# First cross attention: transposed blocks sent through DRAM to their partitions

## The chip, the cores and the metric

The kernel runs on one core of a Trainium2 chip. The core has a matrix engine (TensorE, "PE" in the profile, with its weight loads shown apart as "PEld"), a vector engine (VectorE, "DVE"), a scalar engine (ScalarE, "ACT"), GpSimd ("POOL") and a queue engine (SyncE, "SP") that here only starts transfers. Sixteen DMA engines move the data between DRAM and the on-chip memory SBUF, and within SBUF. SBUF has 128 partitions; a tile of 128 x n elements has n elements in each partition.

The metric is the device time in microseconds. All arithmetic is in float32.

## The reference, cut to what matters

The program is two layers of a perceiver for 16 batches of 64 latent tokens (256 features) that attend to 1024 context tokens per batch. The change touches the first of six blocks, the cross attention of the first layer:

```python
q = jnp.einsum('bsd,dhe->bshe', inputs_q, Wq) + bq      # latents, 64 per batch, 16 heads of 64
k = jnp.einsum('bsd,dhe->bshe', inputs_kv, Wk) + bk     # context, 1024 per batch
v = jnp.einsum('bsd,dhe->bshe', inputs_kv, Wv) + bv
q = q / jnp.sqrt(jnp.asarray(HD, dtype=q.dtype))
scores = jnp.einsum('bqhd,bkhd->bhqk', q, k)
weights = jax.nn.softmax(scores, axis=-1)
ctx = jnp.einsum('bhqk,bkhd->bqhd', weights, v)
out = jnp.einsum('bqhd,hde->bqe', ctx, Wo) + bo
```

Five more blocks follow: a self attention, a small feed-forward block, a second cross attention, a second self attention and a mixture of experts.

## The kernel before

**How the block is tiled.** The keys are never formed: the key weights are multiplied into the queries (`absorb`), so that a score is a product of a query tile with the raw context. A step `s` treats one pair of heads of one batch: 64 latents x 2 heads fill the 128 rows, 1024 context tokens are the columns. There are 8 pairs and 16 batches, so 128 steps. In the same way the values are never formed: the probabilities are multiplied with the raw context (`gather`), and the value weights follow later (`values`).

**One step.** `scores(s)` issues four matmuls (128 x 512 each, tile `x_s` in PSUM), the row maximum (`nmax_x`, L577, DVE), the shift (L581, DVE) and the exponential with its row sum (`pr_x`, L584, ACT). `turn_probs(s)` divides by the sum (L177 and L178, DVE) and transposes within blocks of 32 x 32 (`x_pb`, L593, DVE).

**Why blocks have to move.** `gather` needs the probabilities with the context tokens on the partitions. The vector transpose turns each 32 x 32 block where it stands: what belongs to the partitions 32j to 32j+31 still lies in the partitions 32a to 32a+31, for each of the 4 x 4 pairs (a, j). So after every second step a *pair* w = (2w, 2w+1) of steps is complete in one tile `x_pb` of 128 x 2048 elements (1 MB), and 16 transfers of 64 KB, started by SP at L599, take every block from its 32 partitions to its 32 others, into the tile `x_pT`. `gather(w, c)` then runs 8 matmuls (128 x 256) for each half c of the features: 16 matmuls that read `x_pT` and the context, into `x_po`. There are 64 pairs, so 1024 such transfers.

**The context itself** is transposed in the same manner once for each batch: `turn_context` runs four vector transposes (L547, two for each half of the tokens) into `x_cb`, and 16 transfers of 64 KB (L553) take the blocks into `ctxT`, which `scores` reads. Batch 0 is an exception: PE transposes it (`first_context`). So there are 15 x 16 = 240 transfers here.

**Buffers.** `ctxT` and `x_pT` have two buffers each. `x_cb` and `x_pb` share a pool with two buffers (tag "blocks"). `x_s` has two buffers in PSUM, `x_po` one.

**What sets the order.** In the code a step issues, in this order: `turn_probs(s)`, `scores(s + 1)`, half a `gather` of the pair before, then pieces of `turn_context`, of the next tile's queries, and of the small later stages (self attention and feed-forward of a tile of two batches that is already finished; `small_stages`). That is not the order in which an engine runs them: a scheduler places every instruction on its engine's queue from costs that it estimates itself, except for those that `pin` holds in program order. Each engine then works off its queue in order. An instruction that waits holds everything behind it on that engine. In the second cross attention and what follows, the matmuls are pinned.

**SP's queue** holds nearly all transfers of this block: context loads (L197, two of 512 KB for each batch), the 16 transfers for each `x_pT` and the 16 for each `ctxT`. The weights are loaded from POOL's queue.

Of the kernel before, what the change touches and what calls it, by code (L numbers as in the profile page):

```python
# [8 lines left out]
F32 = mybir.dt.float32  # L9
# [4 lines left out]
P = 128  # L14
# [3 lines left out]
NC = D // P  # L18
N = 1024
NKT = N // P  # L20
# [26 lines left out]
def kernel(  # L47
# [30 lines left out]
    nc = tc.nc  # L78
# [18 lines left out]
    def matmul(*args, **kwargs):  # L97
        ins = nc.tensor.matmul(*args, **kwargs)  # L98
        return pin(ins) if in_order else ins

    def transpose(*args, **kwargs):
        ins = nc.tensor.transpose(*args, **kwargs)  # L102
        return pin(ins) if in_order else ins

    def bank(shape, name):
        return ps.tile(shape, F32, tag="p", name=name)

    def copy(n, dst, src):

        if n % 2:  # L110
            nc.scalar.copy(dst, src)
        else:
            nc.vector.tensor_copy(dst, src)
# [61 lines left out]
    def soft_norm(pr, total, key):  # L175
        inv = small.tile([P, 1], F32, tag="inv", name=f"inv_{key}")
        nc.vector.reciprocal(inv, total)  # L177
        nc.vector.tensor_scalar(pr, pr, inv, None, ALU.mult)  # L178
# [275 lines left out]
    st = ExitStack()  # L454
    two = st.enter_context(tc.tile_pool(name="x_two", bufs=2))
    qkp = st.enter_context(tc.tile_pool(name="x_qk", bufs=3))
    one = st.enter_context(tc.tile_pool(name="x_one", bufs=1))
    ps_s = st.enter_context(tc.tile_pool(name="x_ps_s", bufs=2, space=bass.MemoryType.PSUM))
    ps_o = st.enter_context(tc.tile_pool(name="x_ps_o", bufs=1, space=bass.MemoryType.PSUM))
# [4 lines left out]
    ctxT, qT, qk, kb, pT, acc, pct, oT, probs, blocks = ({} for _ in range(10))  # L464
# [59 lines left out]

    def first_context(g):

        if g == 0:
            ctxT[0] = two.tile([P, NC, 4, NKT, 32], F32, tag="ctxT", name="ctxT_0")  # L530
        h, c = g // 2, g % 2
        src = ctx_tiles[0][h]
        pt = bank([P, 4, P], f"ctxT_0_{g}")
        for k in range(4):
            transpose(pt[:, k, :], src[:, k, c * P : (c + 1) * P], ident)
        for k in range(4):
            copy(g, ctxT[0][:, c, :, 4 * h + k, :], pt[:, k].rearrange("p (a s) -> p a s", a=4))

    def turn_context(b, h):

        if h == 0:
            ctxT[b] = two.tile([P, NC, 4, NKT, 32], F32, tag="ctxT", name=f"ctxT_{b}")
            blocks["c"] = two.tile([P, 4, NC, NKT, 32], F32, tag="blocks", name=f"x_cb_{b}")
        cb = blocks["c"]
        src = ctx_tiles[b][h].rearrange("p k (c j s) -> p k c j s", c=NC, s=32)
        for c in range(NC):
            nc.vector.transpose(  # L547
                cb[:, :, c, 4 * h : 4 * h + 4, :].rearrange("p j k s -> p k j s"), src[:, :, c]
            )
        if h == 1:  # L550
            for a in range(4):
                for j in range(4):
                    nc.sync.dma_start(  # L553
                        out=ctxT[b][32 * j : 32 * j + 32, :, a],
                        in_=cb[32 * a : 32 * a + 32, j],
                    )

    def context_stats(b, k):

# [4 lines left out]
    def scores(s):  # L564
        b, i = divmod(s, NPAIR)
        t, u = divmod(b, 2)
        sc = ps_s.tile([P, N], F32, tag="s", name=f"x_s_{s}")
        for n in range(2):
            for c in range(NC):
                matmul(  # L570
                    sc[:, n * 512 : (n + 1) * 512],
                    lhsT=qk[t, u][:, c, 2 * i : 2 * i + 2, :].rearrange("p h q -> p (h q)"),
                    rhs=ctxT[b][:, c, 2 * n : 2 * n + 2].rearrange("p a k s -> p (a k s)"),
                    start=(c == 0), stop=(c == NC - 1),
                )
        nmax = small.tile([P, 1], F32, tag="nmax", name=f"nmax_x_{s}")
        nc.vector.tensor_reduce(nmax, sc, AX.X, ALU.max, negate=True)  # L577

        add = kb[t][:, u, i : i + 1]
        shift = small.tile([P, 1], F32, tag="shift", name=f"shift_x_{s}")  # L580
        nc.vector.scalar_tensor_tensor(shift, nmax, add, add, ALU.subtract, ALU.add)  # L581
        pr = two.tile([P, N], F32, tag="pr", name=f"pr_x_{s}")
        total = small.tile([P, 1], F32, tag="total", name=f"total_x_{s}")
        nc.scalar.activation(pr, sc, AF.Exp, bias=shift, scale=1.0, accum_out=total)  # L584
        probs[s] = pr, total

    def turn_probs(s):
        pr, total = probs.pop(s)
        soft_norm(pr, total, f"x_{s}")
        w, i = divmod(s, 2)  # L590
        if i == 0:
            blocks[w] = two.tile([P, 4, 2, NKT, 32], F32, tag="blocks", name=f"x_pb_{w}")
        nc.vector.transpose(blocks[w][:, :, i], pr.rearrange("p (j k s) -> p j k s", j=4, s=32))  # L593
        if i == 1:
            pT[w] = two.tile([P, 4, 2, NKT, 32], F32, tag="pT", name=f"x_pT_{w}")
            pb = blocks.pop(w)
            for a in range(4):
                for j in range(4):
                    nc.sync.dma_start(  # L599
                        out=pT[w][32 * j : 32 * j + 32, a], in_=pb[32 * a : 32 * a + 32, j]  # L600
                    )

    def gather(w, c):

# [71 lines left out]
    for g in range(4):  # L676
        first_context(g)
    absorb(0, 0)
    absorb(0, 1)
    first_bias(0)  # L680
    scores(0)
    queries(0, 1)
    pieces = prepare()
    for s in range(NSTEP):
        b, i = divmod(s, NPAIR)
# [3 lines left out]
        if s == NSTEP - PER_TILE + 2:  # L689
# [4 lines left out]
                out=wqo4[:, 0, :].rearrange("p (c n) -> p c n", c=NC),  # L694
                in_=l_wq.rearrange("(c p) n -> p c n", p=P),
            )
            nc.gpsimd.dma_start(
                out=wqo4[:, 1, :].rearrange("p (c n) -> p c n", n=D),
                in_=l_wo.rearrange("(c p) n -> p c n", p=P),
            )  # L700
            raw = {hh: load_half(cpool, hh // 2, hh % 2, "l_ctx") for hh in range(2)}
        if s == NSTEP - 6:
# [4 lines left out]
                cshift, cshift, -1.0, crstd, ALU.mult, ALU.mult  # L707
            )
        turn_probs(s)
        if s + 1 < NSTEP:  # L710
            scores(s + 1)
        if s >= 2:
            gather((s - 2) // 2, s % 2)
        if b + 1 < B and i in (1, 2):
            turn_context(b + 1, i - 1)
# [45 lines left out]
    with ExitStack() as st:  # L761
        one = st.enter_context(tc.tile_pool(name="l_one", bufs=1))
        two = st.enter_context(tc.tile_pool(name="l_two", bufs=2))
# [23 lines left out]
        cnT, kT, qT, vlat, pT, pct, oT, probs = ({} for _ in range(8))  # L787
# [439 lines left out]
        for qq in range(2):  # L1227
            turn_context(qq)
        issue_one()
        turn_latents(0)  # L1230
        for qq in range(2, 4):
            turn_context(qq)
# [4 lines left out]
        keys(2)  # L1237
        issue_one()
        scores(0)
        soften(0, 0)  # L1240
        keys(1)
# [8 lines left out]
        for s in range(NSTEP):  # L1250
# [3 lines left out]
            elif s + 1 < NSTEP:  # L1254
                scores((s + 1) // 2)
            turn_probs(s)
            self_steps(s, early=True)
            if s + 1 < NSTEP:
# [47 lines left out]
    with ExitStack() as st:  # L1306
        one = st.enter_context(tc.tile_pool(name="m_one", bufs=1))
        two = st.enter_context(tc.tile_pool(name="m_two", bufs=2))
# [108 lines left out]
        for n in range(2):  # L1417
            pt = bank([NE, 4, P], f"m_st_{n}")
# [16 lines left out]
        for e in range(NE):  # L1435
            w1, w2 = experts.pop(e)
            h = two.tile([P, NF, P], F32, tag="h", name=f"m_h_{e}")
# [10 lines left out]
            for n in range(2):  # L1448
                pb = bank([P, 512], f"m_pb_{e}_{n}")
                matmul(  # L1450
                    pb, lhsT=k6[0:NE, K6_SEL + e * P : K6_SEL + (e + 1) * P],
                    rhs=slotT[:, n * 512 : (n + 1) * 512], start=True, stop=True,
# [182 lines left out]
```

## Time and profile before

| | us |
|---|---|
| median of 3 runs | 2244.39 (2239.78 to 2245.81) |
| the profiled execution, its own time | 2241.03 |
| its span, first to last instruction | 2239.3 |
| first cross attention, first to last `gather` matmul | 51.2 to 1152 |
| PE busy over the span | 2144.6 (96%) |
| DVE, ACT, POOL busy over the span | 1265.6, 851.2, 310.4 |

Durations are taken from the one profiled execution. "Busy" of PE is modelled and includes the overlap of matmuls that follow each other. In the groups, one 128 x 512 float32 matmul of the code appears as two records, as does every other float32 matmul; "x1024" of `x_s` is 512 matmuls. In a row of a timeline the first column is the start, the second how long the merged group lasted, and the bracket at the end says for how long the engine had been idle and what ended it. A row of windows gives the stretch, its length, and the busy time of PE, PEld, DVE, ACT and POOL with their instruction counts, then the granted TensorE clock, the mean busy share of the DMA engines and the GB/s that they moved.

### The profile page before, as it was taken

To read this page: it belongs to the slowest core of one execution; us is meant where nothing else is said; L and a number is where in the kernel's file an instruction comes from. 1 tells how busy PE (TensorE), PEld (TensorE's weight loads), DVE (VectorE), ACT (ScalarE), POOL (GpSimd) and SP (SyncE) were. 2 spreads that over 40 slices of the span, in tenths; PEclk is the share of its full clock that TensorE was granted. 3 is DMA by queue.
4 is the path that set the end of the run, shared out by engine and by line. 5 is a ranking of instruction groups with operands and counts; after the bars stand their busy time and mean duration, and the time that the engine had idled before them with its cause. 6 is when DMAs were issued, how large, how long until landed. Compare 5 with 4: busy or idle time off the path is not lost. (4 is left out here: it accounts for less than half of the span.)

```text
span 2239.3 us, 32095 instructions
## 1 busy us (share of the span) xinstructions
PE 2144.6 (96%) x11528; PEld 1470.2 (66%) x11528; DVE 1265.6 (57%) x2606; ACT 851.2 (38%) x1633; POOL 310.4 (14%) x302
## 2 busy tenths in 40 slices
PE   7899999999999999999987999999999999998799
PEld 5566666666666666666663656676766666677477
DVE  6755757567475675766526655656565655564311
ACT  2323224333243332333434545555454545443110
POOL 2100001001010010100004222212221212111010
PEclk9999999999999999999989999999999999999799
DMA  7334333343233433443322242222222222112052
GB/s 246 87 96 105 90 76 99 81 105 92 73 100 84 103 91 74 114 108 96 85 78 56 67 140 58 57 58 63 55 63 57 58 57 57 48 48 69 1 170 74
DMA packets 138110, 186.99 MB, mean 84 GB/s; under 512 B 30608, under 2 KB 81296, under 8 KB 137696
## 3 DMA queue, kind: packets, MB, share of 16 engines
q1 hardware_dynamic: 130160, 154.43, 26.6%
q0 software_dynamic: 7792, 30.51, 4.0%
q8 instruction: 92, 1.51, 0.3%
q14 instruction: 66, 0.54, 0.1%
HBM read 67.38 MB, written 1.05 MB: 31 GB/s over the span
## 5 line engine op out<-in xcount | busy, mean ns | idle before, releaser
L98 PE MATMUL x_s<-ctxT,x_qk 128*128 128x512 f32 x1024 | 471.3, 601 | 10.5 <-ACT pr_x L584 10.5
L98 PE MATMUL x_po<-x_pT,ctx 128*128 128x256 f32 x2048 | 459.3, 382 | 4.4 <-DMA x_pT<-x_pb 4.4
L98 PEld LDWEIGHTS x_po<-x_pT,ctx 128*128 128x128 f32 x2048 | 388.6, 191 | 80.4 <-issue 27.0
L98 PEld LDWEIGHTS x_s<-ctxT,x_qk 128*128 128x128 f32 x1024 | 187.1, 190 | 210.0 <-issue 181.5
L577 DVE TENSOR_REDUCE nmax_x<-x_s 128x1 f32<-128x1024 f32 x128 | 156.0, 1218 | 239.0 <-PE x_s L98 238.0
L584 ACT ACTIVATE pr_x<-x_s,shift_x 128x1024 f32<-128x1024 f32 x128 | 142.6, 1114 | 286.8 <-DVE shift_x L581 238.5
L866 POOL TENSOR_TENSOR l_ks<-l_ks,k 128x512 f32<-128x512 f32 x128 | 164.4, 1284 | 578.2 <-DMA l_ks<-l_kr 497.4
L98 PE MATMUL l_pk<-l_cnT,wkv 128*128 128x512 f32 x512 | 232.6, 597 | 3.3 <-ACT l_cnT L821 1.3
L98 PE MATMUL l_po<-l_pT,l_ctx 128*128 128x256 f32 x864 | 199.8, 383 | 0.0
L98 PEld LDWEIGHTS l_po<-l_pT,l_ctx 128*128 128x128 f32 x864 | 161.3, 192 | 21.1 <-issue 0.5
L867 DVE TENSOR_TENSOR l_kT<-l_kT,l_ks 128x512 f32<-128x512 f32 x128 | 89.7, 701 | 147.6 <-POOL l_ks L866 147.0
L98 PEld LDWEIGHTS l_pk<-l_cnT,wkv 128*128 128x128 f32 x512 | 97.6, 192 | 102.2 <-issue 89.5
L593 DVE STREAM_TRANSPOSE x_pb<-pr_x 128x1024 f32<-128x1024 f32 x128 | 157.2, 1236 | 5.9 <-DMA x_pT<-x_pb 2.1
L865 DVE TENSOR_TENSOR l_kT<-l_kr,k 128x512 f32<-128x512 f32 x128 | 89.8, 704 | 98.9 <-ACT l_kr L857 98.2
L857 ACT ACTIVATE l_kr<-l_pk,l_bkv 128x512 f32<-128x512 f32 x128 | 87.7, 685 | 150.7 <-PE l_pk L98 108.9
L618 ACT COPY x_pct<-x_po 128x512 f32<-128x512 f32 x64 | 37.5, 586 | 246.6 <-PE x_po L98 246.6
L178 DVE TENSOR_SCALAR pr_x<-pr_x,inv_x 128x1024 f32<-128x1024 f32 x128 | 100.1, 782 | 3.2
L584 ACT ACT_TABLE_LOAD x42 | 53.9, 1283 | 103.9 <-DVE shift_x L581 103.8
L975 ACT ACTIVATE pr_l<-l_s,nmax_l 128x1024 f32<-128x1024 f32 x64 | 71.3, 1114 | 45.0 <-DVE nmax_l L973 44.6
L102 PEld LDWEIGHTS l_ptp<-ident,pr_l 128*128 128x128 f32 x512 | 57.3, 142 | 41.8 <-issue 18.3
L972 DVE TENSOR_REDUCE nmax_l<-l_s 128x1 f32<-128x1024 f32 x64 | 77.8, 1217 | 7.6 <-PE l_s L98 7.6
L102 PE MATMUL l_ptp<-ident,pr_l 128*128 128x128 f32 x512 | 71.6, 281 | 7.9 <-ACT l_kr L857 4.9
(305 smaller groups left out, 2784.9 us busy)
## 6 DMA issues: line engine op xcount, KB each, us to landing
x_pT<-x_pb SPq DMA_DIRECT2D x1024, 64.0 KB, 2.0
l_ks<-l_kr SPq DMA_DIRECT2D x512, 64.0 KB, 2.0
ctx<-in_context_dram SPq DMA_DIRECT2D x32, 512.0 KB, 5.0
w<-in_m_w_dram POOLq DMA_DIRECT2D x16, 1024.0 KB, 6.3
ctxT<-x_cb SPq DMA_DIRECT2D x240, 64.0 KB, 2.0
l_ctx<-in_context_dram SPq DMA_DIRECT2D x27, 512.0 KB, 4.1
l_ctx_spare<-in_context_dram SPq DMA_DIRECT2D x5, 512.0 KB, 4.2
wq<-in_x_wq_dram POOLq DMA_DIRECT2D x1, 1024.0 KB, 7.4
```

The source lines that it names most:

```text
L98: ins = nc.tensor.matmul(*args, **kwargs)
L102: ins = nc.tensor.transpose(*args, **kwargs)
L178: nc.vector.tensor_scalar(pr, pr, inv, None, ALU.mult)
L577: nc.vector.tensor_reduce(nmax, sc, AX.X, ALU.max, negate=True)
L584: nc.scalar.activation(pr, sc, AF.Exp, bias=shift, scale=1.0, accum_out=total)
L593: nc.vector.transpose(blocks[w][:, :, i], pr.rearrange("p (j k s) -> p j k s", j=4, s=32))
L857: nc.scalar.activation(kr, pk, AF.Identity, bias=bkv[:, i : i + 1])
L865: nc.vector.tensor_tensor(kr2, kr, k4[:, 0, at], ALU.mult)
L866: nc.gpsimd.tensor_tensor(ks, ks, k4[:, 1, at], ALU.mult)
L867: nc.vector.tensor_tensor(kr2, kr2, ks, ALU.add)
L972: nc.vector.tensor_reduce(nmax, sc[h], AX.X, ALU.max, negate=True)
L975: nc.scalar.activation(pr[h], sc[h], AF.Exp, bias=nmax, scale=1.0, accum_out=total[:, 2 * h : 2 * h + 1])
```

## The change

The 16 transfers from SBUF to SBUF are replaced, for `x_pT` and for `ctxT`, by five that go through a DRAM tile (`spread`): one that writes the whole block tile (128 partitions of 8 KB), and four that read it back, each for one a: all 128 partitions of the destination, 512 elements each, taken from 32 consecutive rows of the DRAM tile, where the index j (4 values, stride 512 elements) is the outer one and the row (32 values, stride 2048) the inner one. The read waits for the write. The DRAM pool has two buffers for each of the two uses.

So that a read fills 512 consecutive elements of a partition, `ctxT` has its a index outermost (`[P, 4, NC, NKT, 32]` instead of `[P, NC, 4, NKT, 32]`), and the matmul of the scores reads two runs of 256 elements instead of one of 512. The vector transposes of the context are two for each batch instead of four, each of 1024 elements instead of 512.

```diff
+    dram = st.enter_context(tc.tile_pool(name="x_dram", bufs=2, space=bass.MemoryType.DRAM))
...
+    def spread(dst, src, name, n):
+
+        d = dram.tile([P, 4, src.shape[2]], F32, tag=name, name=f"{name}_{n}")
+        nc.sync.dma_start(out=d, in_=src)
+        for a in range(4):
+            nc.sync.dma_start(
+                out=dst[:, a], in_=d[32 * a : 32 * a + 32].rearrange("i j x -> j i x")
+            )
...
-            ctxT[b] = two.tile([P, NC, 4, NKT, 32], F32, tag="ctxT", name=f"ctxT_{b}")
+            ctxT[b] = two.tile([P, 4, NC, NKT, 32], F32, tag="ctxT", name=f"ctxT_{b}")
...
-        for c in range(NC):
-            nc.vector.transpose(
-                cb[:, :, c, 4 * h : 4 * h + 4, :].rearrange("p j k s -> p k j s"), src[:, :, c]
-            )
+        nc.vector.transpose(cb[:, :, :, 4 * h : 4 * h + 4, :].rearrange("p j c k s -> p k c j s"), src)
         if h == 1:
-            for a in range(4):
-                for j in range(4):
-                    nc.sync.dma_start(
-                        out=ctxT[b][32 * j : 32 * j + 32, :, a],
-                        in_=cb[32 * a : 32 * a + 32, j],
-                    )
+            spread(
+                ctxT[b].rearrange("p a c k s -> p a (c k s)"), cb.rearrange("p j c k s -> p j (c k s)"),
+                "x_cd", b,
+            )
...
-                    rhs=ctxT[b][:, c, 2 * n : 2 * n + 2].rearrange("p a k s -> p (a k s)"),
+                    rhs=ctxT[b][:, 2 * n : 2 * n + 2, c].rearrange("p a k s -> p a (k s)"),
...
-            for a in range(4):
-                for j in range(4):
-                    nc.sync.dma_start(
-                        out=pT[w][32 * j : 32 * j + 32, a], in_=pb[32 * a : 32 * a + 32, j]
-                    )
+            spread(
+                pT[w].rearrange("p a i k s -> p a (i k s)"), pb.rearrange("p j i k s -> p j (i k s)"),
+                "x_pd", w,
+            )
```

More of the change, by code (lines that the diff above doesn't have):

```diff
@@ L522, in absorb @@
                     copy(h, qk[t, u][:, :, 2 * i + h, :], pa[h][:, j, :, u * M : u * M + M])
+    def spread(dst, src, name, n):
[5 more added lines that the diff above has]
+            )
     def first_context(g):
         if g == 0:
-            ctxT[0] = two.tile([P, NC, 4, NKT, 32], F32, tag="ctxT", name="ctxT_0")
+            ctxT[0] = two.tile([P, 4, NC, NKT, 32], F32, tag="ctxT", name="ctxT_0")
         h, c = g // 2, g % 2
@@ L536, in first_context @@
         for k in range(4):
-            copy(g, ctxT[0][:, c, :, 4 * h + k, :], pt[:, k].rearrange("p (a s) -> p a s", a=4))
+            copy(g, ctxT[0][:, :, c, 4 * h + k, :], pt[:, k].rearrange("p (a s) -> p a s", a=4))
     def turn_context(b, h):
         if h == 0:
-            ctxT[b] = two.tile([P, NC, 4, NKT, 32], F32, tag="ctxT", name=f"ctxT_{b}")
+            ctxT[b] = two.tile([P, 4, NC, NKT, 32], F32, tag="ctxT", name=f"ctxT_{b}")
             blocks["c"] = two.tile([P, 4, NC, NKT, 32], F32, tag="blocks", name=f"x_cb_{b}")
@@ L545, in turn_context @@
         src = ctx_tiles[b][h].rearrange("p k (c j s) -> p k c j s", c=NC, s=32)
-        for c in range(NC):
-            nc.vector.transpose(
-                cb[:, :, c, 4 * h : 4 * h + 4, :].rearrange("p j k s -> p k j s"), src[:, :, c]
-            )
-        if h == 1:
-            for a in range(4):
-                for j in range(4):
-                    nc.sync.dma_start(
-                        out=ctxT[b][32 * j : 32 * j + 32, :, a],
-                        in_=cb[32 * a : 32 * a + 32, j],
-                    )
+        nc.vector.transpose(cb[:, :, :, 4 * h : 4 * h + 4, :].rearrange("p j c k s -> p k c j s"), src)
+        if h == 1:
+            spread(
+                ctxT[b].rearrange("p a c k s -> p a (c k s)"), cb.rearrange("p j c k s -> p j (c k s)"),
+                "x_cd", b,
+            )
     def context_stats(b, k):
```

## The prediction

> **What bounds the kernel now.** I read the page first, then the stretch in which this block runs in its steady state, then PE's and SP's rows there.
>
> ```profile
> 100.00:900.00 800.00, 797.62 (x3721) 535.24 (x3720) 498.18 (x1031) 267.15 (x479) 45.77 (x55) 1.00 0.36 91
> ```
>
> PE is busy for 797.6 of 800 us at full clock; DVE has 302 us of air. So nothing here can make the middle of the block faster by more than some 2 us; what can change the time is PE beginning to wait. The idle time that PE has in this block stands in two groups and at the end:
>
> ```profile
> L98 PE MATMUL x_s<-ctxT,x_qk 128*128 128x512 f32 x1024 | 471.3, 601 | 10.5 <-ACT pr_x L584 10.5
> L98 PE MATMUL x_po<-x_pT,ctx 128*128 128x256 f32 x2048 | 459.3, 382 | 4.4 <-DMA x_pT<-x_pb 4.4
> ...
> 1137.02 1.99 PE L98 MATMUL x_out<-wo,x_oT 128*128 128x256 f32 x8
> 1142.12 10.05 PE L98 MATMUL x_po<-x_pT,ctx 128*128 128x256 f32 x32 [3.11 <-DMA x_pT<-x_pb]
> ```
>
> The last `gather` waits 3.11 us for its blocks and then takes 10.05 us; the same 32 records elsewhere take 7.07, so the clock is lower after the pause (granted 0.77 from 1137 to 1152 us). The most that a shorter transfer can win is thus 10.5 + 4.4 + 3.0 = 18 us.
>
> The transfers:
>
> ```profile
> L599 SPq DMA_DIRECT2D x_pT<-x_pb x1024: 507/589/1961, 39.7 to 1140.0; - x171
> ...
> 611.95 10.07 SPq L599 DMA_DIRECT2D x_pT<-x_pb  x16
> ...
> q1 hardware_dynamic: 130160, 154.43, 26.6%
> q0 software_dynamic: 7792, 30.51, 4.0%
> ...
> x_pT<-x_pb SPq DMA_DIRECT2D x1024, 64.0 KB, 2.0
> ctx<-in_context_dram SPq DMA_DIRECT2D x32, 512.0 KB, 5.0
> ...
> out_dram<-m_res SPq DMA_DIRECT2D x8, 128.0 KB, 1.7
> ```
>
> Sixteen starts take SP 10.07 us, and the last lands 2.0 us after it started: about 11.5 us from the last transpose to a complete `x_pT`, set by SP's starts and not by bytes.
>
> **What goes and what it frees.** SP starts 1264 - 395 = 869 transfers fewer (64 + 15 writes and 256 + 60 reads stay), 512 us of SP at 0.589; nobody waits for SP as such, only for what lands. DVE has 60 transposes of 512 elements (0.691 us) replaced by 30 of 1024 (1.24, as in L593): 4 us less, hidden in its air. PE's instructions keep number and shape; two runs of 256 elements instead of one of 512 I price at nothing (a bound: PE reads `x_pT` in runs of 32 for `x_po` at 382 ns for 256 columns, the rate of `x_s`, 601 for 512). ACT gets two more table loads (2 x 1.28 us), hidden. Buffers of `x_pb` come free earlier, after the write. The second cross attention and what follows keep their instructions.
>
> **The new transfer, first by rows.** The write is 1 MB by 128 partitions. A 128 KB store lands in 1.7 us; two context loads started 0.6 us apart, 1 MB together, land 5.6 us after the first start. I take 5.0 for the write (the extra 896 KB at 16 x 21.3 GB/s would give 4.4; the lone 1 MB load by SP, of `k` beside context, took 7.2). SP waits for it, then starts four reads of 256 KB. By the row of the context loads, which have rows of 1 KB over 128 partitions, 1 MB of reads lands in 5.6 us. Sum 5.0 + 0.1 + 5.6 = 10.7 us: a little shorter than now.
>
> **Then by the rule.** The Trainium skill, page "DMA: Bandwidth & Descriptors", section "Why a DMA increments its semaphore by 16 and not by 1", says that a transfer is split over the largest k up to 16 that divides the slowest dimension of both access patterns, and that on SP's queue these are the k lowest-numbered engines. The write has 128 and 128: 16 engines. The reads have 128 partitions on one side, but on the DRAM side `i j x -> j i x` puts j outermost: 4. So each read would run on 4 engines, and all four reads on the same 4. Nothing in this trace tests it: all transfers of before have 32, 64 or 128 outermost (and 30,608 packets under 512 B are about 16 for each of its 1,890 starts, which would fit one closing packet on each engine). A read then moves 1 MB through 4 engines, 256 KB each. How fast is one engine? Queue q0, which only loads from DRAM, moved 30.51 MB in 4.0% of 16 x 2239.3 us: 21.3 GB/s for each busy engine, 12.3 us. Queue q1, mostly SBUF to SBUF, 16.2 GB/s: 16.2 us. The same page's section "Specifications" gives 27 GiB/s for an engine: 9.0 us. I take 11.5, near q0's row because it is the same direction, and a little under it because 12 engines stand aside. With 1.3 us at the ends (the store's 1.7 less its own 0.4 of data) the reads take 12.8, and the whole 5.0 + 0.1 + 12.8 = 17.9 us. I follow the rule: it is stated for just this kind of pattern, and the trace says nothing against it.
>
> **What PE has to cover it.** From the last matmul of a pair's second scores to its `x_pb`, the chain is
>
> ```profile
> L577 DVE TENSOR_REDUCE nmax_x<-x_s 128x1 f32<-128x1024 f32 x128 | 156.0, 1218 | 239.0 <-PE x_s L98 238.0
> L584 ACT ACTIVATE pr_x<-x_s,shift_x 128x1024 f32<-128x1024 f32 x128 | 142.6, 1114 | 286.8 <-DVE shift_x L581 238.5
> ...
> L593 DVE STREAM_TRANSPOSE x_pb<-pr_x 128x1024 f32<-128x1024 f32 x128 | 157.2, 1236 | 5.9 <-DMA x_pT<-x_pb 2.1
> ...
> L178 DVE TENSOR_SCALAR pr_x<-pr_x,inv_x 128x1024 f32<-128x1024 f32 x128 | 100.1, 782 | 3.2
> ```
>
> 1.22 + 1.11 + 0.78 + 1.24, with shift, read of the sum, reciprocal and hand-overs 5.5 us where DVE is free. Now the moved part, which the diff does not show. With 16 starts in a transfer the scheduler put `gather(w)` late: between the end of a pair's scores and its `gather` stand, counted in PE's order with start-to-start times of the timeline (0.86 us for a 128x512 matmul, 0.434 for 256 columns, 0.23 for 128), 21 to 33 us of PE work, 26.6 on average over the eight pairs of a repeated tile. With five starts it draws `gather` forward, one pair nearer: in the new order it is 18.3, 17.6, 18.2, 20.3, 20.5, 18.7, 17.7, 16.9, on average 18.5. One of them written out: half a `gather` (3.5), `x_out` (3.5), scores (3.4), half a `gather` (3.5), scores (3.4), two small transposes (0.9). So 8 us of slack go.
>
> The blocks are there 5.5 + 17.9 = 23.4 us after the scores: 4.9 us late at each of 64 pairs. PE runs in order, so the next scores, and with them the next softmax and the next transfer, stand behind the waiting `gather`. Since 18.5 is about one pair's PE time (17.6), a window usually holds one earlier wait, but sometimes two, which then cover each other in part: between half and all of each wait counts. At three quarters: 64 x 4.9 x 0.75 = 235 us. For 15 batches the context's reads take the same 4 engines for 11.5 us more, and stand in SP's queue next to a pair's write, which cannot start while SP waits for the context's write: 15 x 11.5 x 0.75 = 129. Against this at most 18 us of old waits go; I take 15. Also those four engines alone, with 5 MB of reads for each batch (57.5 us), their sixteenth of the five writes (15.4) and of a batch's context load (3.1), need 76 us where PE needs 70: alone they would bound the block.
>
> Sum against the profiled execution: 2241 + 235 + 129 - 15 = 2590. The median of the runs is 3 us above that execution, inside their own spread of 6; I leave 2590. Lower end: 9.0 us of data, each late time counted at half: 64 x 2.4 x 0.5 + 15 x 9.0 x 0.5 = 144, 2385. Upper end: 16.2 us of data: 64 x 9.6 x 0.75 + 15 x 16.2 x 0.75 = 643, less 15, about 2860.
>
> **Rivals.** (1) *Faster: the reads use all engines.* Then blocks are there after 5.5 + 10.7 = 16.2 us, inside 18.5, and the old waits go: 2241 - 15 = 2226. For it: the row of the context loads, and 13.0 us (18.5 - 5.5) as the point below which no `gather` waits. Against it: the rule. (2) *All engines, but the round trip is slow:* write and reads 7.2 us each like the load of `k`, beside context loads: 14.5, 1.5 us late, 64 x 1.5 x 0.75 = 72, about 2310. Against it: the 1.7 us store shows no dear end of a write. (3) *Hidden anyway:* the transfer is just as long as the new order allows and the early waits of `x_s` stay; 2244. For it: the scheduler may know the price; against it: it placed `gather` by its own estimate, and PE has nothing spare.
>
> **How the numbers follow.** The rule's case 0.86, rival 1 0.09, rival 2 0.02, rival 3 0.03. 2390 to 2860 holds a little over nine tenths of the first case, 0.8 in all. A change of under 0.3% (7 us) is about what a measurement cannot tell from none. Faster by more than that: 0.09; within: 0.03; slower: 0.88.
>
> **What would show it.** `x_po` idle before some 300 us, put down to the DMA of `x_pT`; reads landing 10 us or more after their start, the last of four later than the first; a write landing in about 5; PE's clock dipping after the pauses; under 512 B about 13,000 packets (16 for each write, 4 for each read) and not 17,000. Right mechanism, wrong size: one engine's rate. If the reads land in 3 to 4 us, the prediction is wrong from the rule on, and `x_po` hardly waits.

## The result, and the profile after

| | before | after |
|---|---|---|
| median of the runs, us | 2245.1 | 2676.64 (2673.44 to 2685.01) |
| ratio to before | | 1.193 [1.190, 1.197] |
| span of the profiled execution, us | 2239.3 | 2683.2 |
| first cross attention, first to last `gather` matmul, us | 51 to 1152 | 63 to 1588 |

The change makes the kernel 432 us slower; 2590 had been forecast, in a range of 2390 to 2860. The block of the change takes the whole loss: it ends 436 us later. These lines of the page after answer to those shown of before (costliest groups, the clock's slices, the counts of packets):

```profile
L98 PE MATMUL x_po<-x_pT,ctx 128*128 128x256 f32 x2048 | 555.5, 433 | 360.3 <-DMA x_pT<-x_pd 331.4
L98 PE MATMUL x_s<-ctxT,x_qk 128*128 128x512 f32 x1024 | 471.1, 602 | 2.1 <-ACT pr_x L589 2.1
...
PEclk8888998888898888888888988999999999999799
DMA packets 122836, 269.67 MB, mean 101 GB/s; under 512 B 12912, under 2 KB 48240, under 8 KB 112320
```

Three numbers of the first two lines hold the whole difference. PE stands idle ahead of `x_po` for 360.3 us (4.4 before). The same 2048 records of `x_po` take 555.5 us instead of 459.3, since the clock is lower after most pauses. And `x_s` waits 2.1 us instead of 10.5. So 355.9 + 96.2 - 8.4 = 443.7, and the spans differ by 443.9.

Where the slower records stand, the timeline shows. These are the two halves of two `gather`s; the first half of each comes after a pause:

```profile
408.44 6.04 PE L98 MATMUL x_po<-x_pT,ctx 128*128 128x256 f32 x16 [7.66 <-DMA x_pT<-x_pd]
416.89 3.62 PE L98 MATMUL x_po<-x_pT,ctx 128*128 128x256 f32 x16
441.40 6.62 PE L98 MATMUL x_po<-x_pT,ctx 128*128 128x256 f32 x16 [12.79 <-DMA x_pT<-x_pd]
448.71 3.62 PE L98 MATMUL x_po<-x_pT,ctx 128*128 128x256 f32 x16
```

The granted clock was 0.61 in the first of these rows and 1.00 in the second. Over all 64 pairs, the first half of a `gather` took 2.1 us longer after the 9 pauses of 3 to 5 us, 2.5 longer after the 14 of 5 to 9 us and 2.4 longer after the 16 of more than 9 us, but only 0.1 longer after 5 pauses of 0.5 to 3 us; the second half took 3.62 us in each of these groups. So the price is one for each longer pause, hardly depending on its length: 39 pauses hold 93 of the 96 us.

The middle of the block, as a row of windows:

```profile
100.00:900.00 800.00, 620.61 (x2658) 418.19 (x2658) 369.76 (x741) 195.69 (x342) 35.03 (x41) 0.87 0.33 120
```

PE is busy for 621 us of 800 where it had been for 798, at a clock of 0.87 instead of 1.00. The DMA engines are not busier as a whole (0.33 after 0.36): what is short is a few of them.

The short packets tell how many, if each engine that takes part in a transfer leaves one packet under 512 B. Before, the 1264 transfers of this block would have left 1264 x 16 of the 30,608 short packets, and 10,384 belong to everything else. After: 10,384 + 79 writes x 16 + 316 reads x 4 = 12,912, to the packet. So a read runs on four engines.

One ordinary pair, with no context transfer beside it, in the timeline of the kernel after (first PE, then SP's queue):

```profile
355.80 3.70 PE L98 MATMUL x_s<-ctxT,x_qk 128*128 128x512 f32 x8
...
364.33 3.70 PE L98 MATMUL x_s<-ctxT,x_qk 128*128 128x512 f32 x8
367.87 3.62 PE L98 MATMUL x_po<-x_pT,ctx 128*128 128x256 f32 x16
371.32 1.03 PE L98 MATMUL a_out<-awo,a_oT 128*128 128x256 f32 x4
372.28 1.16 PE L98 MATMUL x_pa<-x_qT,wkT 64*128 64x128 f32 x16
373.37 3.70 PE L98 MATMUL x_s<-ctxT,x_qk 128*128 128x512 f32 x8
382.29 2.30 PE L98 MATMUL x_po<-x_pT,ctx 128*128 128x256 f32 x5 [5.22 <-DMA x_pT<-x_pd]
```

```profile
364.60 0.34 SPq L531 DMA_DIRECT2D x_pd<-x_pb  x1
368.51 2.63 SPq L533 DMA_DIRECT2D x_pT<-x_pd  x4
```

The second scores of this pair are the first row; they end at 359.5. The write starts 5.1 us later, the first read 3.9 us after that, and the blocks are there at 382.3, 13.8 us after the first read. PE has work until 377.1 and waits 5.22 us. One read alone would have 2.7 us of data on each of four engines (32 packets of 2 KB, each 0.084 us at the median of the trace); all four together have 10.8 if they share the same engines, and 2.7 if they don't. 13.8 us says that they share them. The packets themselves confirm it: at the third and fourth pairs of a batch, between 3 and 9 us after the first read's start, 4.2 packets of 2 KB were under way at a time (mean, added up from the trace). All four reads together have no more than four engines. Which four, no run shows.

And the surroundings of a context transfer, in SP's queue of the same kernel:

```profile
395.02 1.84 SPq L533 DMA_DIRECT2D x_pT<-x_pd  x3
398.71 0.32 SPq L531 DMA_DIRECT2D x_cd<-x_cb  x1
410.72 2.44 SPq L533 DMA_DIRECT2D ctxT<-x_cd  x4
413.26 2.01 SPq L531 DMA_DIRECT2D x_pd<-x_pb  x1
418.81 2.11 SPq L197 DMA_DIRECT2D ctx<-in_context_dram  x2
427.75 2.27 SPq L533 DMA_DIRECT2D x_pT<-x_pd  x4
```

The context's write starts at 398.71 but is complete only at 410.7, 12.0 us later instead of 3.9: a pair's four reads had just been started, and the write has a share on each of the engines that they occupy. Its packets show this: three quarters of its 128 packets of 8 KB had started after 3.1 us, and the last quarter, the share of four engines, between 7.9 and 11.3 us. This befalls 6 of the 15 writes of the context, those of every second batch; the others took 3.9 to 5.4 us. The next pair's write, ready at 406.3, stands in SP's queue until 413.26, and it takes 14.5 us, now behind the context's reads. That pair's `gather` starts at 441.40 after a pause of 12.79 us. The write of the first pair is late in nearly every batch: 12.3 us on average over pairs 8 to 59.

### The profile page after: what moved, and what is told of

It reads as the page before. It is cut to its first block, busy times and chain, and to the rows that moved or that the text cites. A ratio compares the mean times of both kernels' runs of the same rounds, so it can differ in the third digit from the quotient of the medians.

```text
span 2683.2 us, 30859 instructions
## 1 busy us (share of the span) xinstructions
PE 2240.7 (84%) x11528; PEld 1534.3 (57%) x11528; DVE 1278.9 (48%) x2576; ACT 854.0 (32%) x1635; POOL 310.0 (12%) x302
## 2 busy tenths in 40 slices
DMA packets 122836, 269.67 MB, mean 101 GB/s; under 512 B 12912, under 2 KB 48240, under 8 KB 112320
## 5 line engine op out<-in xcount | busy, mean ns | idle before, releaser
L98 PE MATMUL x_po<-x_pT,ctx 128*128 128x256 f32 x2048 | 555.5, 433 | 360.3 <-DMA x_pT<-x_pd 331.4
L98 PEld LDWEIGHTS x_po<-x_pT,ctx 128*128 128x128 f32 x2048 | 448.8, 222 | 496.5 <-issue 384.3
L113 DVE COPY x_qk<-x_pa 128x128 f32<-128x128 f32 x128 | 28.3, 277 | 111.5 <-PE x_pa L98 111.5
```

## The experiments

The theory: a read of the changed kernel runs on four engines, always the same four, and PE waits for what this adds to the transfer. The rivals: the way through DRAM costs as such; the context's transfers do most of it; the clock falls for another reason than the pauses. Each kernel was compared with before on the same chip; "alone" below means with the other transfer undone.

**Reads over all engines.** The reads take the same rows that were written, so 128 is outermost on both sides. The permutation of the blocks is thereby left out. PE's order is exactly that of the changed kernel.

```diff
-                out=dst[:, a], in_=d[32 * a : 32 * a + 32].rearrange("i j x -> j i x")
+                out=dst[:, a], in_=d[:, a]
```

> The changed kernel, with the four reads taking row p of the DRAM tile to partition p (128 outermost on both sides) in place of the pattern with j outermost. The blocks thus stay on their partitions: the permutation is left out, so the values differ. Number, size and run length of the transfers are those of the changed kernel, and so is the order of PE. Theory A (a read with 4 outermost runs on 4 DMA engines, and that is the loss): under 512 B some 16,700 packets, last read to gather no longer 11 to 12 us, x_po waits for the transfer under 10 us, clock back near 1; 2215 to 2245 us. Theory B (the way through DRAM is long in itself: a write's receipt, then a read): as the changed kernel, about 2680 us.

Measured: 2246.81 us, ratio 1.0009 [0.9999, 1.0019]. On the page of this kernel:

```profile
L98 PE MATMUL x_po<-x_pT,ctx 128*128 128x256 f32 x2048 | 465.5, 381 | 22.3 <-DMA x_pT<-x_pd 21.4
L98 PE MATMUL x_s<-ctxT,x_qk 128*128 128x512 f32 x1024 | 471.3, 602 | 2.0 <-ACT pr_x L587 2.0
...
DMA packets 126628, 269.68 MB, mean 120 GB/s; under 512 B 16704, under 2 KB 52032, under 8 KB 116112
...
x_pd<-x_pb SPq DMA_DIRECT2D x64, 1024.0 KB, 3.9
x_pT<-x_pd SPq DMA_DIRECT2D x256, 256.0 KB, 4.0
```

16,704 = 10,384 + 79 x 16 + 316 x 16. As many bytes go through DRAM in as many transfers, and the loss is gone; the write lands in 3.9 us and a read in 4.0. So the way through DRAM and the new order of PE cost nothing together. Here 15.1 to 15.6 packets of 2 KB were under way at a time from 2 to 4 us after the first read's start, where the change had 4.2. The clock is back too: `x_po` is at 381 ns with as much traffic through DRAM, so it is not this traffic that lowers the clock. The kernel is just above the range of its expectation (2215 to 2245), and `x_po` waits 22.3 us where under 10 had been expected: `x_s` waits 8.5 us less than before, but `x_po` waits 17.9 us more and takes 6.2 more. The window of the new order, from a pair's scores to its `gather`, is 9 us shorter in the trace (18.1 us of PE work instead of 27.1, pairs 8 to 59), and the first pair of each batch, beside the context's transfer, waits 1.3 us on average.

**The same blocks over 16 engines, with the permutation kept.** One read for each j, whose outer dimension is 32.

```diff
-        for a in range(4):
+        for j in range(4):
             nc.sync.dma_start(
-                out=dst[:, a], in_=d[32 * a : 32 * a + 32].rearrange("i j x -> j i x")
+                out=dst[32 * j : 32 * j + 32], in_=d[:, j].rearrange("(a i) x -> i a x", a=4)
```

> The changed kernel with the four reads cut by j instead of by a: each fills 32 partitions from 32 rows outermost, so that the blocks do arrive where they belong and, by theory A, all 16 engines take part. The scheduler puts a higher price on transfers to 32 partitions: in its new order gather stands 48 to 78 us behind its scores, not 17 to 20. Theory A: no wait for x_pT of the old kind; with two buffers of x_pT and so late a gather the next write's reads wait for PE instead, 2230 to 2330 us. Theory B: the long order covers any round trip as well, so this run alone does not decide; the packets under 512 B do (16,700 against 12,900).

Measured: 2301.07 us, ratio 1.026 [1.023, 1.029]. This mends seven eighths of the loss, inside the expected range. What is left is not a wait for the blocks:

```profile
PE lnT_x L102 <- DVE xn_x L136: 14.3, 2, 7.9
PE x_pv L98 <- ACT x_pct L622: 12.2, 18, 0.7
PE f_p L98 <- DVE hT_f L148: 10.5, 7, 1.7
PE lnT_a L102 <- DVE xn_a L136: 9.8, 6, 1.6
...
PE x_po L98 <- DMA x_pT<-x_pd: 4.5, 1, 4.5
```

In these waits of PE (total, times, longest) `x_po` stands with 4.5 us. The scheduler prices these reads higher and puts a `gather` 49 to 77 us of PE work behind its scores (pairs 8 to 59); five of the last `gather`s stand bare at the end of the block, and small tasks wait for their inputs. That a `gather` had covered these waits before is likely, but not shown.

**One transfer at a time, the other directly as before.** First only the pairs through DRAM, then only the context. PE's order is a new one in both.

```diff
         if h == 1:
-            spread(
-                ctxT[b].rearrange("p a c k s -> p a (c k s)"), cb.rearrange("p j c k s -> p j (c k s)"),
-                "x_cd", b,
-            )
+            for a in range(4):
+                for j in range(4):
+                    nc.sync.dma_start(
+                        out=ctxT[b][32 * j : 32 * j + 32, a], in_=cb[32 * a : 32 * a + 32, j]
+                    )
```

> Only x_pT goes through DRAM, with the reads of the changed kernel; ctxT gets its 16 direct transfers again. By the prediction's terms the context's part (129 us) goes and the 235 of the pairs stay: 2241 + 235 - 15 = 2461; with plain pairs 22 us apart as the trace of the changed kernel has them instead of 17.6, 2241 + 64 x 4.4 = 2520. Theory B gives the same within that. A rival that blames SP, which stands still while it waits for the context's write: 2600 and more would stay.

Measured: 2554.93 us, ratio 1.139 [1.136, 1.142]. It lies 35 us above the 2520 of the expectation and below the 2600 of the rival that blames SP. The 2461 by the prediction's terms lacks the slow clock: `x_po` took 548.1 us here, 89 more than before. The other way round, `x_pT` directly and the context through DRAM:

> Only ctxT goes through DRAM, with the reads of the changed kernel; x_pT gets its 16 direct transfers again. In the order of this kernel gather stands 19 to 28 us behind its scores and needs 18. By the prediction's term 15 x 11.5 x 0.75 = 129 us stay if the four engines are in the way of the pairs' transfers: 2370; if the longer order covers them, 2240 to 2300.

Measured: 2292.28 us, ratio 1.022 [1.019, 1.025]. This lies in the range given for the case that the longer order covers the transfer. So the pairs carry most of it, 311 us, and the context 48. But here the other transfer's 16 starts stand in SP's queue, and with direct pairs the windows are longer (24 us on average). The pair of runs in the changed kernel's own order follows below.

**The number of engines as a dose.** The reads take their rows in an order with o outermost, o = 8 and o = 16, all else the same, PE's order too.

```diff
-                out=dst[:, a], in_=d[32 * a : 32 * a + 32].rearrange("i j x -> j i x")
+                out=dst[:, a], in_=d[:, a].rearrange("(q o) x -> o q x", o=8)
```

> The four reads take their rows in an order with 8 outermost instead of 4 (rows o, o+8, o+16 ... one after another; the order differs from the changed kernel's, so the values do too), PE's order is the changed kernel's. Theory A (each read runs on as many engines as its outermost dimension has, and a gather waits only for what exceeds the window): 8 engines, 10.8 us of data become 5.4, the transfer 3.9 + 0.1 + 5.4 + 1.3 = 10.7, with the softmax 16.2 us after the scores, inside 18.5; only pairs beside a context transfer can wait, up to 5 us each: 2245 to 2300, x_po idle under 60 us, and 13,000 + 319 x 4... that is 64 + 15 writes x 16 and 316 reads x 8 = 3,792 - 1,264 more short packets than the changed kernel. Rival B (the loss is in proportion to the data time of a read, no threshold): a third of 432 us stays, about 2390. Rival C (the order of rows in DRAM costs, not the engines): near the changed kernel, 2600 or more.

> As the run with 8 outermost, but with 16 (rows o, o+16, ... ; values differ from the changed kernel's for that reason), same PE order. Theory A: 16 engines, like the reads of the same rows: 2240 to 2255, x_po idle about 20 us. Rival C (a permuted order of rows in DRAM costs something of its own): above the same-row kernel's 2247 by more than 30 us.

Measured: 2404.89 us with 8, ratio 1.071 [1.067, 1.074], and 2280.66 with 16, ratio 1.016 [1.014, 1.017]. The packets fit both: 14,176 and 16,704 short ones, and up to 8.2 and 15.6 packets of 2 KB under way at a time. Both times fell outside the expectation of the theory as I had put it. The run with 16 (2240 to 2255 expected) is 34 us above the same-row kernel, as the rival has it that gives the order of rows a price of its own. The run with 8 (2245 to 2300 expected) came near the rival of a loss in proportion (2390). I had blamed the context's reads, and tested that by giving only the pairs 8 engines:

```diff
+                in_=d[:, a].rearrange("(q o) x -> o q x", o=8) if name == "x_pd" else d[:, a]
```

> As the run with 8 outermost, but only for the pairs' reads; the context's reads take the same rows of DRAM (128 outermost). The permutations differ from the changed kernel's, so the values do too; PE's order is its order. Theory A (a pair's reads on 8 engines fit the window, and the whole 158 us of the run with 8 outermost came from the context's reads, which lie ahead of the neighbouring pairs' write and reads on the same 8 engines): a pair's blocks are there 5.1 + 3.9 + 0.1 + 6.7 = 15.8 us after its scores, no window is shorter than 16.9 in the middle of the block: 2245 to 2270, x_po idle 20 to 50 us. Rival B (the loss goes with the data time, without a threshold): a third of the 311 us that the pairs alone cost, about 2350.

Measured: 2383.13 us, ratio 1.060 [1.058, 1.063]. On the page of this kernel:

```profile
L98 PE MATMUL x_po<-x_pT,ctx 128*128 128x256 f32 x2048 | 504.4, 403 | 116.8 <-DMA x_pT<-x_pd 100.6
```

So that explanation is wrong too: the pairs' reads alone keep 136 of the 158 us. Where the waits stand tells why. Mean idle time of PE ahead of a `gather`, by the place of the pair in its batch, over pairs 8 to 59, added up from the trace:

| reads: pairs / context | first pair | second | third | fourth |
|---|---|---|---|---|
| all 16 engines / 16 | 1.3 | 0.0 | 0.0 | 0.0 |
| 8 / 16 | 4.5 | 0.0 | 0.7 | 1.4 |
| 8 / 8 | 5.7 | 0.0 | 0.8 | 1.4 |
| 4 / 16 | 8.6 | 0.1 | 4.6 | 3.5 |
| 16 / 4 | 7.8 | 0.0 | 0.0 | 0.0 |
| 4 / 4 (the change) | 13.8 | 0.2 | 4.8 | 3.6 |

No context transfer stands beside the third and fourth pairs. With 8 engines they wait about 1 us on average: from the first read's start to the `gather` that waits for it it takes 9.4 us there (1.9 us of starts and 7.5 behind the last), where I had written 5.4 + 1.3. So there is a threshold, but 8 engines lie just beyond it. (The fourth pair waits only in every second batch; its number is the mean of nothing and about twice as much.) The first pair is another matter: it stands beside the context's load, write and reads even if these use all engines. In the same-row kernel its softmax takes 6.5 us instead of 5.1, its write 5.1 instead of 4.0 and its reads 7.9 instead of 5.6, and with that its slack is used up. From there on its own reads are paid in full: with 8 and 4 engines it is 3.2 and 7.4 us longer from the first read to the `gather`, and PE waits 3.2 and 7.3 us longer.

With 16 outermost it is 34 us slower than with the rows in order, though on as many engines: at ordinary pairs the mean packet of 2 KB took 0.119 us instead of 0.102 (the median stayed at 0.084), and a read landed in 4.7 us instead of 4.0. So the order of rows in DRAM has a small price of its own in that pattern. In the changed kernel the mean packet took 0.089 us and with 8 outermost 0.098, so neither shows such a price; 8 engines with the rows in order were not tried.

**Pairs and context apart, in the same order of PE.** One of the two keeps its reads over four engines, the other takes the same rows.

```diff
+                in_=d[32 * a : 32 * a + 32].rearrange("i j x -> j i x") if name == "x_pd" else d[:, a]
```

> Only the pairs' reads run as in the changed kernel (4 outermost); the context's take the same rows (128 outermost, values differ for that). PE's order is the changed kernel's, and SP has no 16 starts for the context, as it had when the context went directly (2555). Theory A (the pairs' waits are independent of the way of the context): the pairs' 4.9 us less what overlaps, with the slow clock: 2520 to 2570. The prediction's own term for the pairs alone: 2244 + 235 = 2480. Rival (most of the loss needs the context's reads ahead of the pairs'): under 2450.

Measured: 2592.5 us, ratio 1.154 [1.152, 1.156], 22 above the top of the expectation (2520 to 2570) and 112 above the prediction's own term. With the two cases exchanged:

> Only the context's reads run as in the changed kernel (4 outermost); the pairs' take the same rows (128 outermost, values differ for that). PE's order is the changed kernel's. By the prediction's term of the context, 2244 + 129 = 2373. Theory A (a context transfer delays the two neighbouring pairs, but each pair has 5 us of its own to spare against its window, which the changed kernel has not): 2290 to 2350, x_po idle 60 to 100 us. Rival (the context's reads alone cost nothing): 2244 to 2260.

Measured: 2373.18 us, ratio 1.057 [1.055, 1.060]. The costliest group of each, of the pairs alone and of the context alone:

```profile
L98 PE MATMUL x_po<-x_pT,ctx 128*128 128x256 f32 x2048 | 550.7, 430 | 276.7 <-DMA x_pT<-x_pd 240.2
```

```profile
L98 PE MATMUL x_po<-x_pT,ctx 128*128 128x256 f32 x2048 | 495.1, 398 | 119.3 <-DMA x_pT<-x_pd 119.3
```

The context alone costs 126 us, 23 more than the top of the expectation that gave each pair 5 us to spare, and just about what the prediction's term had (129). That agreement is in part luck: the term has waits alone, and the 126 hold 115 us of waits and 36 of slow clock, less 9 that `x_s` gained and what the account below leaves open. It does so although the pairs' own reads use all engines: PE waits only at the first pair of each batch (7.8 us in the table), whose write lies behind the context's reads. The pairs alone cost 346. Together that would be 472; the change costs 432, since both put their waits on the same first pair, which waits 13.8 us and not 8.6 + 7.8.

**Does the clock follow the pauses?** Eight matmuls more ahead of each `gather`, which overwrites them, fed by the first of the four reads. They fill a pause with work that nobody needs.

```diff
+        if c == 0:
+            for k in range(8):
+                matmul(
+                    acc[w][:, c].rearrange("p j m -> p (j m)"),
+                    lhsT=ctx_tiles[b][0][:, k % 4, :P],
+                    rhs=pT[w][:, 0, 0].rearrange("p k s -> p (k s)"),
+                    start=True, stop=True,
+                )
```

> The changed kernel with 8 more matmuls of 256 columns ahead of each gather, fed by the first of the four reads and overwritten by the gather: 64 x 8 x 0.434 = 222 us of PE work that nobody needs. In the new PE order the window from a pair's scores to its first real gather matmul is 20.6 + 3.5 = 24.1 us on average. Theory A (pauses of PE are the loss, and the slower clock follows from the pauses): the 23.4 us of a plain pair fit; 2244 + 222 + some 8 us at each of 15 pairs beside a context transfer = about 2590 (2540 to 2640), so faster than the changed kernel in spite of the added work, x_po at under 400 ns, its idle time under 200 us. Rival D (the slower clock comes from the traffic through DRAM, not from the pauses): x_po stays near 433 ns, 2650 or more. Rival E (the four engines' throughput bounds the loop): the time stays near 2680 with the idle time less by the filler's 222.

Measured: 2688.38 us, ratio 1.197 [1.194, 1.199], on the page of this kernel:

```profile
L98 PE MATMUL x_po<-x_pT,ctx 128*128 128x256 f32 x3072 | 760.0, 407 | 180.6 <-DMA x_pT<-x_pd 170.2
```

Some 222 us of added PE work leave the time almost where it was, and the idle time falls by 180. At the rate of before (459.3 / 2048 each) 3072 records would take 689 us, so 71 us of slow clock are left of 96. The mean time did fall, to 407 ns, but not below 400, and the time did not fall to 2590. The number is that of the rival in which the four engines' throughput bounds the loop, but its mechanism is not shown by that: of four pairs three hardly wait here (0.0, 0.0 and 0.8 us), and the first still waits 9.9. The scheduler also gave another order to PE. So this run shows that the pauses take up work at almost no cost, and it leaves open what the clock alone is worth: the 96 us may lie partly in the shadow of the transfers.

**One account for the runs in this order of PE.** If the loss is pauses plus the slow clock behind them, then the changes of `x_po`'s idle and busy time and of `x_s`'s idle time against before must make the change of the span:

| reads: pairs / context | `x_po` idle | `x_po` busy | `x_s` idle | sum | span |
|---|---|---|---|---|---|
| 16 / 16 | +17.9 | +6.2 | -8.5 | +15.6 | +8.1 |
| 16 / 4 | +114.9 | +35.8 | -8.6 | +142.1 | +130.9 |
| 8 / 16 | +112.4 | +45.1 | -8.6 | +148.9 | +144.6 |
| 4 / 16 | +272.3 | +91.4 | -8.6 | +355.1 | +353.4 |
| 4 / 4 | +355.9 | +96.2 | -8.4 | +443.7 | +443.9 |
| 8 / 8 | +128.8 | +51.6 | -8.6 | +171.8 | +165.4 |
| 16 / 16, every 16th row | +40.4 | +19.0 | -8.6 | +50.9 | +41.5 |

It closes within 12 us in each.

## Why the prediction was right, and where it was off

Sign and mechanism were right, and 2677 lies in the range, which was wide. By its steps:

- **The rule over the row.** The reads run on four engines (12,912 short packets, forecast about 13,000). With 128 outermost the same bytes cost nothing. Going by the row of the context loads would have given rival 1, and the same-row kernel is what that rival describes: 2247 and not 2226, because 8 us of old waits went where 15 had been taken, and the shorter window brought new ones.
- **The transfer.** Write 5.0 forecast, 3.9 measured at an ordinary pair. Reads 12.8 forecast, 13.8 in the pair shown. 17.9 against 17.7 us: so close by luck, since the two errors cancel. The rate of an engine was well taken. At ordinary pairs 2 KB took 0.089 us on the mean, 11.4 us for 256 KB, where 11.5 had been estimated, so the 9.0 and 16.2 us of the two ends were off; starts and ends took 2.4 where 1.3 had been put.
- **The lateness of a pair.** 4.9 us forecast, 4.8 us measured at the third pair of a batch; the fourth waits 0.0 and some 7.5 in turn, 3.6 on average. That a wait often covers the next one shows in the second pair, which waits 0.2.
- **The waits' sum.** Per batch the prediction has 4 x 4.9 x 0.75 + 11.5 x 0.75 = 23.3 us; the trace has 13.8 + 0.2 + 4.8 + 3.6 = 22.4. In all 235 + 129 = 364 against 355.9. The three quarters were an assumption, so the closeness is in part luck. The division is less good: the context is worth 115 us of waits alone, the pairs 272, and they overlap by 31.
- **The four engines as a bound.** 76 us per batch had been reckoned for them alone. A batch takes 4 x 24.7 = 98.9 us in pairs 9 to 56, so by that estimate they would have been busy three quarters of it: that points to transfers standing one behind the other, and not to engines that were full.
- **The gain from old waits.** 15 us forecast, 8.4 came.
- **What was put at nothing.** Two runs of 256 elements cost `x_s` nothing: 602 ns after 601. But the bound given for it compares what can't be compared: 382 ns for 256 columns and 601 for 512 are not the same rate. It is the start-to-start times, 0.434 and 0.86 us, that agree.
- **The lower end** leaves out the 15 us of gain that the forecast and the upper end take off; with them it is 2370. The upper end comes to 2869.
- **The step that failed: the sum had no term for the clock.** The prediction showed a `gather` that took 10.05 instead of 7.07 us after a pause, named the dip as something to look for, and then added up waits only. The slower matmuls are 96 us in the account, 2.4 us for each of 39 pauses of more than 3 us. 2590 misses 2677 by 87: 96 for the clock, 7 for the gain that did not come, less 8 for the waits, and less 8 because the profiled execution lies 7 above the median and the base of the sum 2 above its span.

Rival 2, a slow round trip, is out by the same-row kernel, whose write takes 3.9 and each of whose reads takes 4.0 us; rival 3, hidden anyway, by the result.

## What to carry to other kernels

Before cutting a transfer into fewer and larger ones, read the outermost dimension of both sides of it: with 4 outermost a read of 256 KB took what four engines take, and all such reads queued on the same ones, together with every wide transfer that had a share there. Where PE is the bound and begins to wait for a transfer, add to the waits what the clock takes after them. Count the pauses for it, not their length: here each pause of more than 3 us cost about 2 us of slower matmuls. And look whether the order of the bound engine moves with the transfers: here it left 9 us less to hide the transfer in, without any change to the number or the size of the matmuls.

## What the runs showed of the hardware

- A wide transfer was as slow as its slowest share. A write over 16 engines took 3.9 us alone and 10 to 15 where reads over four engines lay ahead of it, while the mean share of the DMA engines was 0.33: three quarters of its packets went as before, and the last quarter waited.
- Twice the engines did not halve the reads: 13.8 us on four, 9.4 on eight. The starts on SP (1.7 to 1.9 us for four reads on average) and the landing don't shrink.
- The time of 16-engine reads depended on the order of rows: 4.0 us a read with rows in order, 4.7 with every sixteenth row.
- The matmuls after a pause were slower by an amount for each pause. In the five runs of the table with more than 100 us of added pause, a pause of more than 3 us cost 1.8 to 2.4 us on average, and one of 0.5 to 3 us 0.1 to 0.5. For each microsecond of added pause this came to 0.27 us (the change) to 0.40 us (8 engines, whose pauses are shorter).
